# Selective scans on one core: Gelu and Silu on clear steps, A loaded among the scans, seven of 24 products on GpSimd

## The chip, the core and the metric

The kernel runs on one core of a Trainium2 chip. The metric is the device time of one execution in microseconds (us); lower is better. The engines are named as in the profile: PE (TensorE), DVE (VectorE), ACT (ScalarE), POOL (GpSimd) and SP (SyncE, which here only issues transfers).

## The reference

Eight images of 56 x 56 positions with 192 channels go through four layers. Layer 0 splits the channels: one half goes through three convolutions, the other through a layer norm, a projection, a depthwise convolution with Silu and a selective scan in four directions, then a gate and a projection. Layers 1 and 2 are selective scans in four directions with a layer norm. Layer 3 is a shifted-window attention with an MLP (Gelu). What takes the time is the scan, which all of layers 0 to 2 have, for each of 4 directions, 192 channels d and 16 states n:

```
delta = softplus(dts @ dt_proj + bias)                     # per channel and position
h = exp(delta * A) * h + (delta * u) * B                   # A = -exp(A_logs), per (d, n)
y = sum over n of h * C        + D * u
```

## The kernel before

**Units and steps.** A unit is one direction of one layer of one image over a chunk of 784 positions (CK); each image and layer has 4 x 4 of them, 384 in all. Inside a unit, 192 channels x 16 states are cut into 24 steps, each one tile of 128 partitions (32 channels x 4 states) x 784 positions: two halves of the channels (h), four groups of states (sg), three groups of channels (j). So there are 9216 steps, and `s % 24` says where in its unit a step is, `s % 12` where in its half.

**One step.** All engines' work is written out in one loop in `run` (the calls are recorded through wrappers, so nearly all instructions carry line L109). For step t:

- `make`: ACT writes exp(delta * A) into `ps_x`, one of two PSUM tiles, from `dsp` (delta spread over the states); POOL writes `db` = `usp` x `bt`, one of four tiles.
- one iteration later, DVE does the scan along the positions. Its initial value is a column of `state`. In most steps the result goes back into `ps_x`, and DVE multiplies it by `ct` (C) into `hc`. In the other steps, which I call product steps, the scan's result goes straight into `hc`.
- two iterations after `make`, ACT copies the last column of the scan's result into `state`, and in product steps POOL multiplies `hc` by `ct` in place. POOL's product therefore stands in its queue behind the `db` of two steps later, and it overwrites a tile that ACT's copy has to have read.
- after every third step PE sums the three `hc` over the states into `ps_y` (`add_up`). In step 5 of each half ACT copies `ps_y` of the half before into the sum over directions (`merge`, the copy act<-ps_y).

In the kernel before, the product steps are every fourth: t % 4 == 3, six of 24.

**Preparing a half.** `prepare` works out delta for the next half of 12 steps: PE multiplies, ACT applies softplus to two tiles of 392 positions, POOL multiplies delta by u into `du`, SP spreads both over the states into `dsp` and `usp`.

**Tables.** Exp and Ln are in one set of tables on ACT; Softplus, Gelu and Silu are each in another. So each softplus, Gelu or Silu has a table load ahead of it and one behind it (`use_ln_exp`). `table_time` holds these tasks until a step where they may be issued; before, those are the steps with s % 4 in (1, 2).

**Other work.** Everything else (the convolutions, norms, attention and MLP) is written as generators in three queues: `ahead` (`prepare`), `urgent` (norms and projections between layers) and `back` (the front of the next image, the attention of the last). After each step's own instructions the loop takes pieces of `ahead` as far as they go, then of `urgent`, then of `back`, as long as an estimated budget of PE and ACT time per step (SPARE, MOST) isn't used up. When a half or a chunk is needed at once, `need` forces the queues. The order on each engine is the order of these calls; no scheduler changes it.

**Start and end.** `constants` loads the constants before anything else. A of the three layers is loaded there by 48 DMAs on POOL's queue (L264), and ACT (L268) and DVE (L269) turn each into -exp(A_logs). After the last scan the attention of the last image runs alone.

Of the kernel before, what the change touches and what calls it, by code (L numbers as in the profile page):

```python
# [32 lines left out]
AF = mybir.ActivationFunctionType  # L33
# [19 lines left out]
NSG = N // SN  # L53
NG = C // G * NSG
# [84 lines left out]
class Net:  # L139
# [56 lines left out]
    def constants(self, ctx):  # L196
        nc, cp = self.nc, self.cp
        self.vt = self.const("vec", [CH, NV])
        self.ident = cp.tile([128, 128], F32, name="ident")
        make_identity(nc, self.ident)  # L200
        self.ones = cp.tile([CH, CH], F32, name="ones")
        nc.vector.memset(self.ones, 1.0)
        self.eps = cp.tile([128, 1], F32, name="eps")
        nc.vector.memset(self.eps, EPS)
        self.blk = self.const("blk", [CH, CH])
        self.esum = cp.tile([128, G], F32, name="esum")
        nc.vector.reduce_sum(
            self.esum, self.ident.rearrange("p (d n) -> p d n", n=SN), axis=AX.X
        )


        self.wx = []
        for l in range(3):
            R = RANK[l]
            wx = cp.tile([CH, 2, 2, 4 * N + 2 * R], F32, name=f"wx{l}")
            for k in range(K):
                d, at = k // 2, 4 * N + k // 2 * R
                src = self.a[f"wx{l}"][:, :, k, :]
                nc.sync.dma_start(
                    out=wx[:, :, k % 2, 2 * N * d : 2 * N * d + 2 * N], in_=src[:, :, R:]  # L220
                )
                nc.scalar.dma_start(out=wx[:, :, k % 2, at : at + R], in_=src[:, :, :R])
                for c in range(2):
                    at = VAT[f"dtb{l}"] + c * K + k
                    nc.gpsimd.dma_start(
                        out=self.dtw[:1, l, k, CH * c : CH * c + CH],
                        in_=self.a["vec"][:, at : at + 1].rearrange("p o -> o p"),
                    )
            self.wx.append(wx)
            nc.sync.dma_start(out=self.dtw[1 : 1 + R, l], in_=self.a[f"dtw{l}"])  # L230

        with self.tc.tile_pool(name="setup", bufs=1) as sp:

            rstd = sp.tile([CH, 3], F32, name="rstd")
            at = VAT["bn1_v"]
            nc.scalar.activation(rstd, self.vt[:, at : at + 3], AF.Sqrt, bias=self.eps[:CH])
            nc.vector.reciprocal(rstd, rstd)
            self.bns = cp.tile([CH, 3], F32, name="bns")
            self.bnb = cp.tile([CH, 3], F32, name="bnb")
            at = VAT["bn1_g"]  # L240
            nc.vector.tensor_mul(self.bns, self.vt[:, at : at + 3], rstd)
            t = sp.tile([CH, 3], F32, name="bnt")
            at = VAT["bn1_m"]
            nc.vector.tensor_copy(t, self.vt[:, at : at + 3])
            for i in (1, 2):
                nc.vector.tensor_sub(t[:, i : i + 1], t[:, i : i + 1], self.v(f"conv{i}_b"))
            nc.vector.tensor_mul(t, t, self.bns)
            at = VAT["bn1_b"]
            nc.vector.tensor_sub(self.bnb, self.vt[:, at : at + 3], t)


            self.dsum = dsum = cp.tile([CH, 3, 2], F32, name="dsum")
            self.A = []
            for l in range(3):
                at = VAT[f"D{l}"]
                d = self.vt[:, at : at + 2 * K].rearrange("p (c k) -> p c k", k=K)
                nc.vector.reduce_sum(dsum[:, l, :], d, axis=AX.X)
                A = cp.tile([128, K, C // G, NSG], F32, name=f"A{l}")
                src = self.a[f"A{l}"].rearrange(
                    "(d s n) (k j q) -> q s d n k j", s=NSG, n=SN, k=K, q=4  # L260
                )
                for q in range(4):
                    for sg in range(NSG):
                        nc.gpsimd.dma_start(  # L264
                            out=A[32 * q : 32 * q + 32, :, :, sg], in_=src[q, sg]
                        )
                A = A.rearrange("p k j s -> p (k j s)")
                nc.scalar.activation(A, A, AF.Exp)  # L268
                nc.vector.tensor_scalar_mul(A, A, -1.0)  # L269
                self.A.append(A)  # L270


            ls = sp.tile([CH, 2], F32, name="ls")
            at = VAT["ls"]
            nc.vector.tensor_scalar_min(ls, self.vt[:, at : at + 2], math.log(100.0))
            nc.scalar.activation(ls, ls, AF.Exp)
            self.scm = cp.tile([CH, 2, 3], F32, name="scm")
            at = VAT["hm"]
            for c in range(2):
                nc.vector.tensor_scalar_mul(  # L280
                    self.scm[:, c, :], self.vt[:, at : at + 3], ls[:, c : c + 1]
                )
            self.ln1024 = cp.tile([CH, 1], F32, name="ln1024")
            nc.vector.memset(self.ln1024, 10.0 * math.log(2.0))

    def l3_constants(self):

# [105 lines left out]
    def table_time(self):  # L393


        while self.step % 4 not in (1, 2) and not self.forced:
            yield 1

    def other_table(self, func, *tiles):
# [415 lines left out]
    def run(self):  # L815
        nc = self.nc
# [13 lines left out]
        for i in range(NC):  # L830
            self.urgent.append(Task(self.after(-1, i)))
        self.urgent.append(Task(self.columns(0)))
        self.state = self.s1.tile([128, NG], F32, name="state")
        self.B_, self.C_, self.spread = {}, {}, {}

# [2 lines left out]
        ]  # L838
        S = len(steps)
        half = NG // 2  # L840
        self.step = 0
        self.ahead.append(Task(self.prepare(units[0], 0, 0)))
        self.need(("half", 0))
        self.ahead.append(Task(self.prepare(units[0], 1, half)))
        for sg in range(NSG):
            self.load_bc(units[0], sg)
        made, weighed, copies = {}, {}, deque()
        left = dict.fromkeys(self.load, 0.0)
        for s in range(S + 8):
# [5 lines left out]
            t = s + half + 1  # L855
            if t < S and t % half == 0:
                self.ahead.append(Task(self.prepare(*steps[t][:2], t)))
            if s < S and s % half == 0:
                self.need(("half", s))
                U = steps[s][0]  # L860
                if s % (16 * NG) == 0:
                    if U.l == 0:
                        self.begin_image(U.b)
                    self.dd = self.s1.tile([CH, 2, CH], F32, name="dd")
                    for c in range(2):
                        nc.scalar.activation(
                            self.dd[:, c, :], self.ident[:CH, :CH], AF.Copy,
                            scale=self.dsum[:, U.l, c : c + 1],
                        )

            t = s - 2
            if 0 <= t < S and not steps[t][0].last:
                U, h, sg, j = steps[t]
# [5 lines left out]
            t = s - 1  # L879
            if 0 <= t < S:  # L880
                U, h, sg, j = steps[t]
                x, db = made[t]
                pool = t % 4 == 3
                hc = self.s6.tile([128, CK], F32, name="hc")
                hs = hc if pool else x
                sense = slice(None) if U.k < 2 else slice(None, None, -1)
                nc.vector.tensor_tensor_scan(
                    hs[:, sense], x[:, sense], db[:, sense],
                    0.0 if U.first else self.at_state(h, sg, j), ALU.mult, ALU.add,
                )  # L890
                if not pool:
                    nc.vector.tensor_mul(hc, hs, self.C_[U, sg])
                made[t] = hs
                weighed[t] = hc
            t = s - 2
            if 0 <= t < S and t % 4 == 3:
                U, h, sg, j = steps[t]
                nc.gpsimd.tensor_mul(weighed[t], weighed[t], self.C_[U, sg])
            t = s - 4
            if 0 <= t < S and t % 3 == 2:  # L900
                U, h, sg, j = steps[t]
# [6 lines left out]
            while self.piece(self.ahead):  # L908
                pass
            self.spend(left, before)  # L910
            for queue in (self.urgent, self.back):
                while min(left["PE"], left["ACT"]) > 0.0 and self.piece(queue):
                    before = self.spend(left, before)

            t = s - 4
            if 0 <= t < S and t % NG >= half and t % 3 == 2:
                n = t // NG + 1
# [484 lines left out]
MOST = {"PE": 3.4, "ACT": 2.5, "DVE": 1.6, "POOL": 3.0}  # L1402


def view(t, k, c, i, n):

    if k % 2 == 0:
        return t[:, c, i : i + n]
    return t.rearrange("p c (h w) -> p c w h", w=HW)[:, c, i // HW : (i + n) // HW, :]
# [120 lines left out]
```

## Time and profile before

| | |
|---|---|
| median of 3 runs | 27071.03 us (27067.4 to 27074.87) |
| the profiled execution: its own time | 27060.61 us |
| its span (first to last instruction) | 27058.8 us |
| busy share: DVE, POOL, PE, ACT | 89%, 85%, 68%, 64% |
| first scan starts, last scan ends | 181.1 us, 26410.6 us |
| mean granted PE clock | 0.756 |

A group of instructions in the profile reads: line, engine, operation, tiles written <- tiles read, sizes, count | busy us in all, mean ns of one | idle us of the engine just before them, and what ended most of that idle time. A wait reads: waiting engine and tile <- what it waited for: us in total, times, longest us. In the timeline each line has the start, the length, and in brackets the idle time ahead of it.

### The profile page before, as it was taken

The page shows a single profiled execution, that of the slowest core. Times are in us where ns is not written, and L with a number is a line of the kernel's source. Part 1 is how long each engine was busy: PE and PEld are TensorE (multiplying, and loading weights), DVE is VectorE, ACT ScalarE, POOL GpSimd, SP SyncE. Part 2 cuts the span into 40 slices and gives each one's busy share as a digit, 9 for nine tenths or more (in the row PEclk, how much of TensorE's full clock was granted, in tenths as well). Part 3 has the DMA queues.
Part 4 walks back from the last instruction along what each step waited for, and adds up shares of the span by engine and source line. Part 5 has one row for each costly group of instructions (what it writes and reads, how often), then busy time and mean ns, then how long its engine had stood idle before and what let it go on. Part 6 is the DMA issues. An engine that isn't in the chain of part 4 may idle for free. (4 is left out here: it accounts for less than half of the span.)

```text
span 27058.8 us, 260255 instructions
## 1 busy us (share of the span) xinstructions
PE 18495.3 (68%) x76788; PEld 6432.0 (24%) x76788; DVE 24122.4 (89%) x18972; ACT 17211.8 (64%) x30893; POOL 23054.4 (85%) x13199
## 2 busy tenths in 40 slices
PE   6675567676676666766667676677766776676657
PEld 2221122222222222222222222222212222222114
DVE  5999999999999899999999999989999899999991
ACT  4655566665666666666666666666666666666655
POOL 5888988888888888888888888888888888888991
PEclk7776677777777777777777777777777777777777
DMA  4555565556555565555655556555565555555550
GB/s 96 135 138 124 133 136 133 126 127 139 135 132 127 125 144 132 132 126 129 142 131 132 127 131 140 133 129 127 131 140 131 129 128 135 134 129 129 130 132 25
DMA packets 1503447, 3472.21 MB, mean 128 GB/s; under 512 B 310618, under 2 KB 503219, under 8 KB 1502020
## 3 DMA queue, kind: packets, MB, share of 16 engines
q1 hardware_dynamic: 1496452, 3455.15, 56.0%
q8 instruction: 606, 9.93, 0.1%
q0 software_dynamic: 3072, 0.31, 0.1%
q14 instruction: 821, 6.73, 0.1%
q10 hardware_dynamic: 2496, 0.09, 0.0%
HBM read 1457.23 MB, written 147.89 MB: 59 GB/s over the span
## 5 line engine op out<-in xcount | busy, mean ns | idle before, releaser
L109 POOL TENSOR_TENSOR db<-usp,bt 128x784 f32<-128x784 f32 x9216 | 16832.7, 1857 | 161.8 <-DMA usp<-du 129.3
L109 DVE TENSOR_TENSOR_SCAN ps_x<-ps_x,state,db 128x784 f32<-128x784 f32 x5184 | 9569.7, 1846 | 834.0 <-ACT state L109 358.7
L109 ACT ACTIVATE ps_x<-dsp,A 128x784 f32<-128x784 f32 x9216 | 8464.1, 919 | 2496.9 <-DVE hc L109 2190.5
L109 PE MATMUL ps_y<-hc,esum 128*32 128x392 f32 x36864 | 6959.3, 641 | 1147.3 <-POOL hc L109 780.6
L109 DVE TENSOR_TENSOR hc<-ps_x,ct 128x784 f32<-128x784 f32 x6912 | 6739.5, 975 | 651.4 <-DVE ps_x L109 11.0
L109 POOL TENSOR_TENSOR hc<-hc,ct 128x784 f32<-128x784 f32 x2304 | 4254.4, 1847 | 2696.2 <-ACT state L109 2104.5
L109 ACT COPY state<-ps_x 128x1 f32<-128x1 f32 x5184 | 831.4, 160 | 4659.5 <-DVE hc L109 4637.4
L109 DVE TENSOR_TENSOR_SCAN hc<-ps_x,state,db 128x784 f32<-128x784 f32 x1728 | 3181.7, 1841 | 161.6 <-POOL db L109 58.2
L109 DVE TENSOR_TENSOR_SCAN ps_x<-ps_x,db 128x784 f32<-128x784 f32 x1728 | 3085.0, 1785 | 261.1 <-ACT state L109 149.1
L109 PEld LDWEIGHTS ps_y<-hc,esum 128*32 128x32 f32 x36864 | 1630.6, 130 | 6096.7 <-issue 3212.3
L109 PE MATMUL ps_y<-act,ident 96*96 96x392 f32 x2304 | 1612.2, 835 | 1760.4 <-ACT act L109 1746.4
L109 PE MATMUL ps_p<-act,act 13*96 13x392 f32 (+1 forms) x3072 | 1513.0, 605 | 1116.6 <-ACT s L109 210.4
L109 POOL TENSOR_TENSOR du<-delta,act 96x784 f32<-96x784 f32 x768 | 1567.9, 2042 | 201.3 <-ACT delta L109 198.7
L109 PE MATMUL ps_p<-act,wx 96*88 96x392 f32 (+1 forms) x1536 | 985.8, 778 | 686.9 <-ACT delta L109 394.0
L109 ACT ACT_TABLE_LOAD x896 | 1149.6, 1283 | 34.4 <-PE ps_p L109 18.9
L390 ACT ACT_TABLE_LOAD x897 | 1150.9, 1283 | 15.6
L109 PEld LDWEIGHTS ps_y<-act,ident 96*96 96x96 f32 x2304 | 465.0, 223 | 2603.1 <-ACT act L109 2056.6
L109 DVE TENSOR_TENSOR_SCAN hc<-ps_x,db 128x784 f32<-128x784 f32 x576 | 1025.8, 1781 | 58.8 <-ACT state L109 38.0
L109 PEld LDWEIGHTS ps_p<-act,act 13*96 13x96 f32 (+1 forms) x3072 | 465.4, 180 | 2033.6 <-issue 373.5
L109 ACT COPY act<-ps_y 96x784 f32<-96x784 f32 x768 | 928.0, 1208 | 8.5 <-PE ps_y L109 8.5
L109 PE MATMUL ps_p<-xip,diag 96*96 96x448 f32 x2016 | 864.0, 580 | 94.4 <-ACT delta L109 94.3
L109 ACT COPY state<-hc 128x1 f32<-128x1 f32 x1728 | 328.6, 190 | 883.6 <-DVE hc L109 880.4
(212 smaller groups left out, 18126.0 us busy)
## 6 DMA issues: line engine op xcount, KB each, us to landing
dsp<-delta SPq DMA_DIRECT2D x2304, 392.0 KB
usp<-du SPq DMA_DIRECT2D x2304, 392.0 KB
bt<-bcd SPq DMA_DIRECT2D x1536, 392.0 KB
ct<-bcd SPq DMA_DIRECT2D x1536, 392.0 KB
wf<-in_wf SPq DMA_DIRECT2D x128, 288.0 KB
wf<-wf2d SPq DMA_DIRECT2D x128, 288.0 KB
bcd<-bcx SPq DMA_DIRECT2D x256, 134.8 KB
szd<-sz SPq DMA_DIRECT2D x56, 336.0 KB
```

The lines of the kernel that those rows point to most:

```text
L109: return call(out, *args, **k)
L390: self.tc.nc.scalar.preload_act_table_set(LN_EXP)
```

## The change

Three things are changed together.

- **A.** Only layer 0's A is loaded in `constants`, by 16 DMAs on ACT's queue; its exp and sign (`decay`) come just ahead of the first exp of a scan. The loads of the other two, 32 DMAs, are a task in `urgent` (`decays`), four at a time on SP's queue, followed by the same exp and sign.
- **Products.** The product steps are seven of 24: t % 24 in (2, 6, 9, 13, 16, 20, 23).
- **Steps for tables.** A step is clear if neither it nor the one before is a product step and it isn't step 5 of its half. Softplus may be issued on clear steps; Gelu and Silu on clear steps that aren't among the first three of a half. While a softplus waits for its step, no piece of `urgent` and `back` is taken; in the iteration after one in which a Gelu or Silu waited, `back` is taken ahead of `urgent`.

```diff
-                for q in range(4):
-                    for sg in range(NSG):
-                        nc.gpsimd.dma_start(
-                            out=A[32 * q : 32 * q + 32, :, :, sg], in_=src[q, sg]
-                        )
-                A = A.rearrange("p k j s -> p (k j s)")
-                nc.scalar.activation(A, A, AF.Exp)
-                nc.vector.tensor_scalar_mul(A, A, -1.0)
-                self.A.append(A)
+                self.logs.append([
+                    (A[32 * q : 32 * q + 32, :, :, sg], src[q, sg])
+                    for q in range(4) for sg in range(NSG)
+                ])
+            for out, part in self.logs[0]:
+                nc.scalar.dma_start(out=out, in_=part)
...
+    def decay(self, l):
+
+        self.nc.scalar.activation(self.A[l], self.A[l], AF.Exp)
+        self.nc.vector.tensor_scalar_mul(self.A[l], self.A[l], -1.0)
+        self.done.add(("A", l))
+
+    def decays(self, l):
+        for n, (out, part) in enumerate(self.logs[l]):
+            self.nc.sync.dma_start(out=out, in_=part)
+            if n % 4 == 3:
+                yield 1
+        yield 4
+        self.decay(l)
...
-        while self.step % 4 not in (1, 2) and not self.forced:
+
+        ahead = self.rank == 2
+
+        def clear(s):
+            late = s % (NG // 2) == 5 or not ahead and s % (NG // 2) < 3
+            return not (late or products(s) or products(s - 1))
+
+        while not self.forced and not clear(self.step):
+            if ahead:
+                self.quiet = self.step
+            else:
+                self.wanted = self.step
             yield 1
...
+        for l in (1, 2):
+            self.urgent.append(Task(self.decays(l)))
...
         self.need(("half", 0))
+        self.decay(0)
...
+                    self.need(("A", U.l))
...
-                pool = t % 4 == 3
+                pool = products(t)
...
-            if 0 <= t < S and t % 4 == 3:
+            if 0 <= t < S and products(t):
                 U, h, sg, j = steps[t]
                 nc.gpsimd.tensor_mul(weighed[t], weighed[t], self.C_[U, sg])
...
-            for queue in (self.urgent, self.back):
-                while min(left["PE"], left["ACT"]) > 0.0 and self.piece(queue):
+            both = self.urgent, self.back
+            for queue in both[::-1] if self.wanted == s - 1 else both:
+                while min(left["PE"], left["ACT"]) > 0.0 and self.quiet < s and self.piece(queue):
...
+def products(t):
+
+    return t % 24 in (2, 6, 9, 13, 16, 20, 23)
```

More of the change, by code (lines that the diff above doesn't have):

```diff
@@ L252, in constants @@
             self.dsum = dsum = cp.tile([CH, 3, 2], F32, name="dsum")
-            self.A = []
+            self.A, self.logs = [], []
             for l in range(3):
@@ L258, in constants @@
                 A = cp.tile([128, K, C // G, NSG], F32, name=f"A{l}")
+                self.A.append(A.rearrange("p k j s -> p (k j s)"))
                 src = self.a[f"A{l}"].rearrange(
@@ L840, in run @@
         half = NG // 2
-        self.step = 0
+        self.step, self.quiet, self.wanted = 0, -1, -1
         self.ahead.append(Task(self.prepare(units[0], 0, 0)))
         self.need(("half", 0))
+        self.decay(0)
         self.ahead.append(Task(self.prepare(units[0], 1, half)))
```

## The prediction

> **What bounds the kernel now.** I read the busy line of the page first, then busy time by stretch, then the costliest groups, then the timeline of a quiet stretch, and last the waits of VectorE (DVE), GpSimd (POOL) and ScalarE (ACT). The busy line:
>
> ```profile
> PE 18495.3 (68%) x76788; PEld 6432.0 (24%) x76788; DVE 24122.4 (89%) x18972; ACT 17211.8 (64%) x30893; POOL 23054.4 (85%) x13199
> ```
>
> Busy time by stretch (DVE, ACT and POOL are the third to fifth figures after the length); the first scan starts at 181 us, the last ends at 26410.6:
>
> ```profile
> 0.00:182.00 182.00, 65.47 (x132) 24.72 (x132) 9.75 (x57) 53.65 (x105) 65.62 (x89) 0.82 0.35 48
> 500.00:26411.00 25911.00, 17761.60 (x72959) 6064.67 (x72958) 23856.51 (x18598) 16653.52 (x29556) 22764.07 (x12938) 0.76 0.58 132
> 26411.00:27058.00 647.00, 462.49 (x3096) 270.95 (x3096) 76.56 (x168) 357.84 (x967) 53.64 (x65) 0.77 0.10 26
> ```
>
> So there is a head of 181 us, a loop of 26229 us with 9216 steps (2.846 us each), and a tail of 647 us. In the loop DVE is busy 92% and POOL 88%: a change that hands work from one to the other can swap the bound. The groups it moves:
>
> ```profile
> L109 POOL TENSOR_TENSOR db<-usp,bt 128x784 f32<-128x784 f32 x9216 | 16832.7, 1857 | 161.8 <-DMA usp<-du 129.3
> L109 DVE TENSOR_TENSOR hc<-ps_x,ct 128x784 f32<-128x784 f32 x6912 | 6739.5, 975 | 651.4 <-DVE ps_x L109 11.0
> L109 POOL TENSOR_TENSOR hc<-hc,ct 128x784 f32<-128x784 f32 x2304 | 4254.4, 1847 | 2696.2 <-ACT state L109 2104.5
> L109 POOL TENSOR_TENSOR du<-delta,act 96x784 f32<-96x784 f32 x768 | 1567.9, 2042 | 201.3 <-ACT delta L109 198.7
> ```
>
> DVE's timeline in a stretch without a wait (start, length):
>
> ```profile
> 13020.55 1.85 DVE L109 TENSOR_TENSOR_SCAN ps_x<-ps_x,state,db 128x784 f32<-128x784 f32 x1
> 13022.51 0.97 DVE L109 TENSOR_TENSOR hc<-ps_x,ct 128x784 f32<-128x784 f32 x1
> 13023.40 1.85 DVE L109 TENSOR_TENSOR_SCAN ps_x<-ps_x,state,db 128x784 f32<-128x784 f32 x1
> ...
> 13026.24 1.84 DVE L109 TENSOR_TENSOR_SCAN hc<-ps_x,state,db 128x784 f32<-128x784 f32 x1
> 13028.00 1.83 DVE L109 TENSOR_TENSOR_SCAN ps_x<-ps_x,state,db 128x784 f32<-128x784 f32 x1
> ```
>
> A step whose product stays on DVE takes 2.84 us there (13020.55 to 13023.40), one whose product goes to POOL 1.76 us (13026.24 to 13028.00). At that pace the loop would take 6912 x 2.84 + 2304 x 1.76 = 23690 us; 2540 us are lost. Some 440 us of that are DVE's other work, about 1570 us waits (its idle of 2218 us in the loop less 6912 x 0.094 us of turnaround before products), the rest lost overlap around them. DVE's longest waits in the loop, then POOL's:
>
> ```profile
> DVE ps_x L109 <- ACT state L109: 414.5, 295, 5.4
> DVE ps_x L109 <- ACT ps_x L109: 336.8, 240, 5.2
> DVE ps_x L109 <- POOL db L109: 148.8, 65, 14.2
> POOL hc L109 <- ACT state L109: 1981.3, 1105, 6.3
> ```
>
> DVE waits mostly for ACT, which is late with the next exp. POOL waits 1981 us before its products for the copy of a state out of the same tile: there it is ahead and is held to DVE's pace.
>
> What makes ACT late is shown best by a Gelu that falls in the step of a merge copy; ACT, then DVE:
>
> ```profile
> 4853.15 0.81 ACT L109 COPY act<-ps_y 96x784 f32<-96x784 f32 x1
> ...
> 4856.36 2.17 ACT L109 ACTIVATE hid<-hid 128x2352 f32<-128x2352 f32 x1
> 4858.54 1.28 ACT L390 ACT_TABLE_LOAD   x1
> 4859.84 1.76 ACT L109 ACTIVATE ps_x<-dsp,A 128x784 f32<-128x784 f32 x2
> ```
> ```profile
> 4860.86 1.86 DVE L109 TENSOR_TENSOR_SCAN ps_x<-ps_x,state,db 128x784 f32<-128x784 f32 x1 [4.59 <-ACT ps_x L109]
> ```
>
> I sorted the scans' waits for ACT by what ACT had run in the 7 us before: 191 us in 55 waits had a Gelu, 82 us in 49 a Silu, 93 us in 66 a softplus in a merge copy's step, 118 us another softplus, 521 us none of these (about 100 us of it before 430 us).
>
> **Two rules of the Trainium skill.** "ScalarE: Activation LUTs", What ACT_TABLE_LOAD costs: a switch of table is a load of about 1283 ns and a drain of about 1380 ns. The load agrees (1283 ns mean of both table groups), the drain doesn't show: at 4858.54 the load starts as the Gelu ends, and the exp follows its end by 0.02 us. I go by the trace: Gelu 4.76 us with both loads, Silu 4.18, softplus 3.48. "GPSIMD Engine Reference", Specifications: GpSimd shares SBUF interfaces with VectorE, and contends with VectorE instructions that have two SBUF inputs. The scans and products here read one tensor in PSUM and one in SBUF, and the change adds no others; POOL's product ranges only from 1825 to 1985 ns. So I leave all durations as they are.
>
> **The change, part by part.** The sum is made against the profiled execution, 27060.6 us (span 27058.8); the median of the runs is 10 us above it, and I add those at the end.
>
> *A among the scans.* 48 loads of A on POOL's queue (46.7 us at 0.98 each) go; ACT waits for them until 63 us, and its chain to the first scan starts only then. In their place are 16 loads on ACT's queue. The nearest row is ACT's loads of wx, 0.62 us each: 10 us, so ACT is free at about 22 us instead of 63: -40. Bounds: with 2.5 us per load (four times wx's pieces) nothing is gained. The other 32 are issued by SP behind about 100 scans, up to 12 in a row between dsp and usp; SP issues about one DMA a step (10683 in all) at 0.5 to 2 us each, and what is late behind them is the next usp or bt: between 0 and 30 us, +10. The three exps (0.28 us) and products (0.21 us) of A are moved, not added; each stands on ACT four steps or more behind its loads, so the exps queued behind it have nothing to wait for.
>
> *Seven products in 24 steps.* The step pattern becomes 2, 6, 9, 13, 16, 20, 23. DVE: 384 steps go from 2.84 to 1.76 us: -415. (In busy time 384 x 0.975 = 374.)
>
> POOL gets 384 products of 1.80 us from start to start: +691. It had 26229 - 22940 = 3290 us idle in the loop, so most of it fits, but not all. Per 24 steps the clean pace is: DVE 17 x 2.84 + 7 x 1.76 = 60.6; POOL 31 x 1.82 + 2 x 2.2 (du) = 60.8, and its other work 1.5 (DVE's other work 1.1). Today it is 61.7 against 59.0. POOL can't build up a lead: its product of step p stands behind db of p+2 and waits for the scan of p, so it has two dbs in hand there, no more. In a stretch of four steps between products it needs 9.1 us and DVE 10.3; in the new stretches of three 7.3 against 7.4, and with a du 9.5. The built order puts 308 du into the stretch 23-2 and 212 into 13-16 (softplus on steps 1 and 15), 156 behind step 13 and 76 behind 5, in stretches of four. With softplus on step 1, counted from the start of scan 0: the product of 23 ends at 2.1, db 2 at 3.9, du at 6.1, db 3 at 7.9; scan 2 starts at 5.7 and, as its product is POOL's, scan 3 could start at 7.4. Today that scan has 1.05 us in hand in the median (and under 0.12 in 14%), with a step of 2.84 ahead; it loses 1.08. So half of these 520 stretches begin to wait: about 0.3 us on average, 156 us. As much again for POOL's 576 small products (0.64 to 0.97 us) and DMA waits, whose slack goes in the stretches of three: +300 in all. Bounds: 0 (DVE's ACT waits give POOL the time anyway) to +700 (every POOL microsecond shows).
>
> *Gelu and Silu on clear steps.* No product starts there, no merge copy, and softplus's own steps are left out. On a clear step two full steps (5.68 us) pass between the exp ahead of the event and the scan that needs the next exp; less exp, state copy and exp (0.92 + 0.16 + 0.92) that leaves 3.68 us: softplus (3.48) fits, Silu exceeds it by 0.5 and Gelu by 1.1. In the built order the events in a merge copy's step fall from 105 (23 Gelu, 81 softplus) to 1, and those one step behind another from 46 to 14. Gelu: 191 to 56 x 1.1 = 62: -130. Silu: 82 to 37: -45. Softplus off step 5: -80. Together -255; bounds -100 to -330. Back work that is held while a softplus waits comes later in the same 24 steps; eight Gelus lie behind the last scan in both programs, so the tail is not longer. If that cover is gone, PE and ACT get bunched work: up to +100, in the range.
>
> Sum: -40 + 10 - 415 + 300 - 255 = -400: 26660.6, with the 10 us 26670.
>
> **Rivals.** (1) *All of it comes through*: POOL's new work hides wholly, as its 12% idle suggests: 26370. Against it: equal clean paces. (2) *The transfer cancels itself*: the DVE gain of 415 comes back as waits for db (+700): 27070. (3) *POOL becomes the bound and ends slower*. Its place is the product that waits for the state copy: 2000 us of idle that POOL needs to stay behind DVE and ACT. If the idle doesn't shrink, the loop grows by all 691 us, less 40: 27720. The time is 691 - 40 less what the idle shrinks by: my sum needs it to shrink by 1050 (3290 to 2240); under 590 the kernel is slower. For it: seven synchronisations instead of six; against it: six in ten of these waits end with POOL ahead, and a slower POOL simply waits less. (4) *The change doesn't do what it says*: the built order shows the steps as named above, so I give it nothing.
>
> **Numbers.** A measurement of this kernel tells 0.2% (54 us) from no change. My case 0.68, its own range 26400 to 27000; rival 1 0.10; rival 2 0.10; rival 3 0.12. Below 27017: my case and rival 1, with the edge of both: 0.80; within 0.2% 0.08; slower 0.12. The range 26330 to 27070 takes in rival 1 and the near side of rival 2.
>
> **What would show it.** First scan near 141 us. DVE busy near 23750, POOL near 23710. POOL's wait for state copies down from 1981 us to about 1100; DVE's waits for db up from 225 us to about 500; its waits for ACT down by 250, none of 4 us behind a Gelu. I am wrong if DVE waits for db over 900 us, if POOL's idle stays above 2600, or if the first scan doesn't move.

## The result: 1.3% slower, and the profile after

The changed kernel takes 27418.95 us (median of 4 runs, 27409.67 to 27423.9) against 27072.95 for the kernel before: ratio 1.013, 95% interval 1.0113 to 1.0146. The prediction was 26670, and its range ended at 27070. The profiled execution of the changed kernel has a span of 27407.3 us; its first scan starts at 144.0 us and its last ends at 26755.6.

The busy line, and busy time by stretch (head, loop, tail; DVE, ACT and POOL are the third to fifth figures after the length):

```profile
PE 18596.9 (68%) x76788; PEld 6535.9 (24%) x76788; DVE 23809.3 (87%) x18588; ACT 17085.8 (62%) x30893; POOL 23713.7 (87%) x13535
```
```profile
0.00:145.00 145.00, 64.43 (x132) 24.56 (x132) 9.44 (x55) 52.83 (x103) 18.85 (x41) 0.78 0.30 57
500.00:26756.00 26256.00, 17832.38 (x72834) 6159.02 (x72834) 23507.82 (x18193) 16509.28 (x29530) 23427.04 (x13298) 0.74 0.56 130
26756.00:27407.00 651.00, 463.40 (x3096) 271.05 (x3096) 76.71 (x168) 356.81 (x967) 53.62 (x65) 0.77 0.10 26
```

DVE lost 313 us of work and POOL gained 659, about as planned, and both now stand at 87%. The head is 37 us shorter, the tail 4 longer. The loss is in the loop: 26612 us instead of 26229. The groups that were to move kept their durations (975, 1845, 2038 ns); what changed is the idle time ahead of them:

```profile
L109 POOL TENSOR_TENSOR db<-usp,bt 128x784 f32<-128x784 f32 x9216 | 16868.1, 1857 | 351.3 <-DMA usp<-du 296.5
L109 DVE TENSOR_TENSOR hc<-ps_x,ct 128x784 f32<-128x784 f32 x6528 | 6364.9, 975 | 611.8 <-DVE ps_x L109 15.6
L109 POOL TENSOR_TENSOR hc<-hc,ct 128x784 f32<-128x784 f32 x2688 | 4959.7, 1845 | 2164.2 <-ACT state L109 1718.9
L109 POOL TENSOR_TENSOR du<-delta,act 96x784 f32<-96x784 f32 x768 | 1565.4, 2038 | 335.4 <-ACT delta L109 262.1
```

POOL's wait for usp ahead of db rose from 129 to 296 us. In the loop alone DVE's longest waits are these, and ACT's and PE's that matter here:

```profile
DVE ps_x L109 <- POOL db L109: 479.5, 488, 8.4
DVE ps_x L109 <- ACT ps_x L109: 434.8, 225, 10.1
DVE hc L109 <- ACT state L109: 333.5, 253, 7.3
...
DVE hc L109 <- POOL db L109: 70.4, 50, 7.2
```
```profile
ACT bcx L109 <- PE ps_p L109: 613.8, 169, 12.6
ACT ps_x L109 <- DMA dsp<-delta: 341.4, 221, 6.9
```
```profile
PE ps_p L109 <- DMA act<-u0d: 489.9, 28, 19.6
```

DVE waits 550 us for db instead of 225. The lines of ACT and PE were 152, 102 and 190 us in the kernel before: late loads, and a copy of ACT's (`bcx`) behind one of them. The loop can be split as in the prediction. From scan to scan a step still takes 2.84 us in the median with its product on DVE and about 1.76 without (1.757 before, 1.765 now); at that pace the loop would take 23270 us, 415 less than before, and what is lost beyond that rose from about 2540 to 3340.

**Where the stall behind u0 comes from.** In the loop u0, the input of the next image, is loaded 28 times. In the kernel before, every one of these loads was followed by two or three steps with a softplus in them, and only then by the projection that reads it; in the changed kernel none is. Kernel before, timeline (SPq is SP's queue), then the changed kernel:

```profile
9963.60 0.57 SPq L713 DMA_DIRECT2D act<-u0d  x1
...
9966.88 0.88 ACT L109 ACTIVATE delta<-ps_p 96x392 f32<-96x392 f32 x2
...
9969.68 2.86 PE L109 MATMUL ps_p<-act,wx 96*76 96x392 f32 x4 [8.88 <-DMA act<-u0d]
...
9972.58 0.48 ACT L109 COPY bcx<-ps_p 76x392 f32<-76x392 f32 x1 [1.24 <-PE ps_p L109]
```
```profile
10049.28 0.58 SPq L736 DMA_DIRECT2D act<-u0d  x1
10055.08 2.87 PE L109 MATMUL ps_p<-act,wx 96*76 96x392 f32 x4 [18.07 <-DMA act<-u0d]
...
10057.99 0.48 ACT L109 COPY bcx<-ps_p 76x392 f32<-76x392 f32 x1 [11.97 <-PE ps_p L109]
...
10059.48 1.86 DVE L109 TENSOR_TENSOR_SCAN ps_x<-ps_x,state,db 128x784 f32<-128x784 f32 x1 [9.77 <-ACT state L109]
```

The load takes 5.8 us from issue to the first matmul in the second case. What differs is what ACT has queued: before, three exps and a softplus; after, the copy `bcx` stands next in the queue, and the state copy and exp that the scan needs stand behind it. DVE stood idle for over 8 us ahead of a scan 10 times before and 33 times after. In 28 of the 33 the cause is such a load, at the end of layer 2, where the next image's input comes in. Together these 28 stalls last 270 us.

### The profile page after: what moved, and what is told of

Its sections match the earlier page's. It is cut to its first block, busy times and chain, and to the rows that moved or that the text cites. A ratio compares the mean times of both kernels' runs of the same rounds, so it can differ in the third digit from the quotient of the medians.

```text
span 27407.3 us, 260324 instructions
## 1 busy us (share of the span) xinstructions
PE 18596.9 (68%) x76788; PEld 6535.9 (24%) x76788; DVE 23809.3 (87%) x18588; ACT 17085.8 (62%) x30893; POOL 23713.7 (87%) x13535
## 5 line engine op out<-in xcount | busy, mean ns | idle before, releaser
L109 POOL TENSOR_TENSOR db<-usp,bt 128x784 f32<-128x784 f32 x9216 | 16868.1, 1857 | 351.3 <-DMA usp<-du 296.5
L109 DVE TENSOR_TENSOR_SCAN ps_x<-ps_x,state,db 128x784 f32<-128x784 f32 x4896 | 9038.8, 1846 | 1005.5 <-POOL db L109 376.6
L109 PE MATMUL ps_y<-hc,esum 128*32 128x392 f32 x36864 | 6837.1, 634 | 1097.7 <-POOL hc L109 666.5
L109 DVE TENSOR_TENSOR hc<-ps_x,ct 128x784 f32<-128x784 f32 x6528 | 6364.9, 975 | 611.8 <-DVE ps_x L109 15.6
L109 POOL TENSOR_TENSOR hc<-hc,ct 128x784 f32<-128x784 f32 x2688 | 4959.7, 1845 | 2164.2 <-ACT state L109 1718.9
L109 DVE TENSOR_TENSOR_SCAN hc<-ps_x,state,db 128x784 f32<-128x784 f32 x2016 | 3714.9, 1843 | 368.2 <-ACT state L109 202.6
L109 DVE TENSOR_TENSOR_SCAN ps_x<-ps_x,db 128x784 f32<-128x784 f32 x1632 | 2914.8, 1786 | 328.1 <-ACT ps_x L109 163.9
L109 POOL TENSOR_TENSOR du<-delta,act 96x784 f32<-96x784 f32 x768 | 1565.4, 2038 | 335.4 <-ACT delta L109 262.1
L109 DVE TENSOR_TENSOR_SCAN hc<-ps_x,db 128x784 f32<-128x784 f32 x672 | 1197.7, 1782 | 151.7 <-ACT state L109 138.4
L109 ACT COPY state<-hc 128x1 f32<-128x1 f32 x2016 | 384.0, 190 | 785.0 <-DVE hc L109 779.3
```

The costliest lines, as they stand in the source:

```text
L109: return call(out, *args, **k)
```

## The experiments

All ratios are against the kernel before, measured alongside (27055 to 27073 us).

**A alone (e4).** The kernel before with the part on A and nothing else.

> The kernel before with the first part of the change alone (A loaded on ACT's queue and among the scans). Both theories: first scan at 144 us instead of 181, the loop as before: 27036 us. If the 32 loads on SP's queue delay dsp and usp, up to 30 us of that is lost: 27066.

Measured: 27049.62 us, ratio 0.9996 (0.9987 to 1.0005). The first scan starts at 142.5 us, but the loop is 20 us longer, so some 10 of the 38 us reach the end, less than a measurement tells.

**The hold and the load of u0 (e1, e3).** I call it the hold that other work is kept back while a softplus waits. e1 takes the hold away; e3 keeps it and puts three iterations between the load of u0 and its reader.

```diff
# e1
-                while min(left["PE"], left["ACT"]) > 0.0 and self.quiet < s and self.piece(queue):
+                while min(left["PE"], left["ACT"]) > 0.0 and self.piece(queue):
# e3, in after(), behind the DMA out of u0
+                if g >= 0:
+                    yield 3
```

> The changed kernel, but other work is no longer held while a softplus waits for its step. Theory S (the hold moved the u0 loads behind the softplus, so ACT's copy of the projection stands right behind a load that has not landed; 26 stalls of about 9.8 us = 255 us): in the built order 12 of 28 copies again have a softplus ahead of them, so about 12 x 9 = 110 us come back: 27310 us, and about 14 stalls over 8 us instead of 29. Rival P (seven products make POOL the bound): no change, 27420. Rival H (the hold protects the softplus from work ahead of it on ACT): slower, 27500 or more.

> The changed kernel with three iterations between the issue of a u0 load and the projection that reads it. Theory S: the 10 us stalls behind the 28 loads go, -230 us: 27190 us; ACT's wait of bcx for PE falls from 670 us to about 220. Rival P: nothing changes, 27420 us, since DVE's waits for db stay at 568 us.

Measured: e1 27266.05 us, 1.0076 (1.0061 to 1.0091); e3 27250.37 us, 1.0069 (1.0054 to 1.0084). Against the changed kernel e1 gains 153 us and e3 169. In e3 the gaps over 8 us fall from 33 to 5; of the 270 us of stalls, 100 come back as other waits or lost overlap. In e1 12 of the 28 loads have a softplus behind them again, as foreseen, but 16 stall as before, and 26 gaps over 8 us are left, not about 14: some 120 us of its gain are the 12 stalls, the rest has no account. So the hold isn't alone in taking the cover away. The new steps for softplus do it too: in e5 below, which has no hold, 22 of the 28 loads stall.

**Six against seven products (e2, e6, e5).** e2 is the changed kernel with `t % 4 == 3`, e6 is e2 with e3's three steps, e5 is the kernel before with seven products and a table rule to fit, without hold and without the part on A. The rule for tables looks at the product steps, so e2 and e6 also move softplus, Gelu and Silu to other steps.

```diff
# e2, e6
-    return t % 24 in (2, 6, 9, 13, 16, 20, 23)
+    return t % 4 == 3
```

> The changed kernel with the six product steps of before (every fourth). Theory S: the stalls behind the u0 loads stay (the copy follows the load with no softplus between), DVE has 384 more steps of 2.84 instead of 1.76 us (+415), its waits for db fall from 568 us to about 250: 27420 + 415 - 320 = 27510 us. Rival P: the seventh product is what costs; six bring the time to that of before less the earlier start, 27040 us or less.

> The changed kernel with six product steps and three iterations between a u0 load and its projection: both suspected losses are undone, the earlier start and the steps for Gelu and Silu stay. Theory M with S: 27198 less 20 to 28 stalls of 9 us = 26980 us, faster than the kernel before by 0.3%. Rival R (the hold itself costs): 27060 or more.

> The kernel before with the seven product steps alone; tables on any step that neither is nor follows a product step (the rule of before, carried over to the new pattern), no hold, A as before. Theory M (the seventh product costs more than it saves: DVE saves 415 us of steps, but waits for db and for late dsp grow by more): 27060 + 210 = 27270 us, DVE's waits for db over 480 us, ACT's waits for dsp over 300. Rival Q (the product move gains and the rules for the tables lose): 26800 us or less.

Measured: e2 27198.28 us, 1.005 (1.0033 to 1.0067); e6 27035.29, 0.9989 (0.9982 to 0.9995); e5 27336.72, 1.01 (1.0085 to 1.0115). With u0's stall and without it, the kernel with seven products takes 215 to 221 us more than the one with six. In e2 DVE's scans wait 170 us for db instead of 568 (whole execution), POOL for usp 125 instead of 296, ACT for dsp 120 instead of 358. But the scans' waits with a Gelu ahead fall as well, from 191 to 94 us, because the table rule gives Gelu other steps: the 220 us are not the seventh product's alone. e2 lies between its two forecasts, e6 55 us above its own and e5 67 above its nearer one.

In e6 the scans' waits with a Gelu ahead are 95 us instead of the 191 of the kernel before and those with a Silu 19 instead of 82, yet with A the whole gains only 27 us: the waits without a table event at the steps around a merge copy rose from about 45 to 130.

**POOL later, or loads earlier (e7, e9, e10, e16).** A ring is the set of tiles that a name uses in turn. e7 issues POOL's product one iteration later. e9 (on e3) and e10 (on e6) give usp and dsp rings of five tiles, and let the loads for j = 1 and 2 be issued a step earlier; e16 is e10 with the hc ring back at eight.

```diff
# e7
-            t = s - 2
+            t = s - 3
             if 0 <= t < S and products(t):
# e9, e10 (e16: HCS = 8 and bcx from s1)
-        delta = self.s2.tile([CH, CK], F32, name="delta")
+        delta = self.s1.tile([CH, CK], F32, name="delta")
...
-            while j and self.step < start - 4 + j:
+            while j and self.step < start - 5 + j:
...
-                s = self.s4.tile([128, CK], F32, name=name)
+                s = self.spreads[name].tile([128, CK], F32, name=name)
...
-HCS = 8
+HCS = 7
```

> The changed kernel with POOL's product issued one iteration later, behind db of three steps ahead instead of two. Theory L (POOL is held to DVE with two dbs in hand at every product, and is late after each): one more db in hand, DVE's waits for db fall from 568 to about 250 us and ACT's for dsp from 358 to about 150: 27170 us. Rival W (POOL has too much work whatever its order, and PE now waits longer for hc): DVE's waits for db stay over 450, PE's waits for hc rise above 667 us, the time is 27420 or more.

Measured: 27641.22 us, 1.0209 (1.0193 to 1.0224). The signs of rival W came (DVE's scans wait 818 us for db, PE 1527 for POOL's hc). But what POOL lacks first isn't time: now with three dbs in hand, it gets to a db sooner and finds its usp not there. These waits are from the whole execution of e7:

```profile
POOL db L109 <- DMA usp<-du: 1127.6, 386, 9.4
```

The theory that POOL needs a longer lead fell. What counts is when these loads are issued. With rings of four, the loads for j = 1 and 2 of the next half take tiles that the current half frees in its steps 9 and 10, four steps ahead of their use. The changed kernel's timeline shows such loads; the first line is POOL's db of steps 21 and 22, and the usp at 14803.10 is that for j = 2:

```profile
14794.12 3.66 POOL L109 TENSOR_TENSOR db<-usp,bt 128x784 f32<-128x784 f32 x2
...
14797.22 1.43 SPq L1049 DMA_DIRECT2D dsp<-delta  x1
...
14798.70 1.09 SPq L807 DMA_DIRECT2D bcd<-bcx  x1
...
14799.84 2.51 SPq L1001 DMA_DIRECT2D bt<-bcd  x1
14802.45 0.55 SPq L1001 DMA_DIRECT2D ct<-bcd  x1
14803.10 0.55 SPq L1049 DMA_DIRECT2D usp<-du  x1
...
14803.74 0.56 SPq L1049 DMA_DIRECT2D dsp<-delta  x1
...
14810.27 5.55 POOL L109 TENSOR_TENSOR db<-usp,bt 128x784 f32<-128x784 f32 x3 [2.34 <-DMA usp<-du]
...
14811.26 1.75 ACT L109 ACTIVATE ps_x<-dsp,A 128x784 f32<-128x784 f32 x2 [2.70 <-DMA dsp<-delta]
```

From issue to use it is 7.2 us, and both POOL and ACT stand idle for it: 209 of the 384 units have such a wait of POOL at step 2, 79 before. The tile itself was free at 14797.78, when POOL had ended the db of step 22. SP, which issues in the order of the program, came to the load 5.3 us later: ahead stood the dsp for j = 1, a store of `bcx`, and `bt` and `ct` (B and C for the next unit). I compared, for each of the 240 late loads of usp for j = 2, its issue with the end of the db that frees its tile: the issue comes 4.2 us later in the median, and `bt` and `ct` take 3.1 us of that on average. The loads for j = 1 do go out as soon as their tile is free (0.03 us), and only 10 of them are late. So what makes a load late is mostly its place in SP's queue, not the ring.

> Base: e3 (seven products, projection three steps after its load of u0; 27250, +188 over before). Here usp and dsp have rings of five tiles instead of four (delta one instead of two, hc seven instead of eight, to make room), and a spread load j may be issued a step earlier. Theory L2 (the seventh product costs time because the loads of usp and dsp for j = 2 come late: their slot is freed by the db and exp of the half before, only two or three steps ahead): POOL's waits for usp fall from about 300 us to under 120, ACT's for dsp from about 360 to under 120, and the time falls by 120 us or more, to 27130 or below. Theory B (POOL's stretch of three steps with du is too short for its work, whoever frees a tile): usp and dsp waits fall, but DVE's waits for db stay above 450 us and the time stays within 60 us of 27250.

> Base: e6 (six products, projection three steps after u0; 27035, -27 against before). The same larger rings. Theory L2: with six products these waits are small (about 125 us each), so at most 60 us are gained: 26975 to 27035. Theory B: within 30 us of 27035. If the smaller hc ring costs anything, it shows here as more than 27065.

Measured: e9 27053.99 us, 0.9997 (0.9989 to 1.0006), 196 less than e3. e10 27058.43, 1.0 (0.9991 to 1.0008), no gain against e6 (23 us more). The db group of e3, then of e9:

```profile
L109 POOL TENSOR_TENSOR db<-usp,bt 128x784 f32<-128x784 f32 x9216 | 16863.4, 1856 | 344.3 <-DMA usp<-du 273.4
```
```profile
L109 POOL TENSOR_TENSOR db<-usp,bt 128x784 f32<-128x784 f32 x9216 | 16867.6, 1857 | 77.3 <-DVE ps_x L109 43.5
```

The waits for usp are gone, and ACT's for dsp (354 us) with them. So late loads are what cost these 196 us, and theory L2 held for seven products in that; its reason, the tile freed too late, holds for few of them. In e9 the load for j = 2 goes out in the median 11.6 us ahead of its use instead of 7.2. Ring and place in the queue were changed together; a run with rings of four and the loads moved ahead of `bt` and `ct` wasn't made. DVE's scans still wait 416 us for db in e9 (536 in e3), under B's 450. With six products the smaller hc ring seems to have cost what the loads brought (e10, waits of DVE), and e16 shows what stood in its place (waits of ACT):

```profile
DVE hc L109 <- PE ps_y L109: 291.0, 115, 6.6
```
```profile
ACT bcx L109 <- DMA bcd<-bcx: 278.6, 75, 9.8
```

> As e10 (six products, larger rings; 27058) with the hc ring back at eight (bcx one tile instead of two to make room). DVE's wait for PE's ps_y (291 us in e10, about 2 in e6) goes: 26900 to 27000 if nothing else takes its place, within 30 us of 27058 if DVE then waits for ACT instead. Set beside e13 it tells whether seven products are worth more than six once loads, u0 and events are seen to: theory B (POOL short of time) says six stay even or ahead, the clean count of DVE says seven by 100 or more.

Measured: 27146.01 us, 1.0036 (1.0023 to 1.0049), a miss: the wait for ps_y went (2 us), but with one tile `bcx` waits for the store of the one before. So what larger rings alone are worth to six products stays open.

**POOL's time (e11, e12).** The same pair, seven on e3 and six on e6, with the du product left out and usp loaded from delta.

```diff
...
-                    nc.gpsimd.tensor_mul(
-                        like(du, k), like(delta, k), view(self.bufs[U.g % 2], k, h, i * CK, CK)
-                    )
...
```

> Base: e3 with seven products. The du product (768 of 2.04 us on POOL) is left out: usp is loaded from delta. Its purpose is the difference to the next run. Theory B (POOL lacks time: 31 db or C products of 1.82 and two du in 60.6 us): without du POOL needs 56.4 us per 24 steps against DVE's 60.6, so seven products are faster than six by 200 us or more (of the clean 415), where with du they are slower by 215; db waits under 200 us. Theory M (a product on POOL hands over at a price, whatever time POOL has: the scan after it follows 1.76 us behind, ACT and PE have to keep up): seven stay slower than six by over 50 us.

> Base: e6 with six products, du left out in the same way. POOL had time to spare with six, so little is gained: theory B says 26950 to 27035 and seven products below it by 200 us or more; theory M says that this run stays the faster of the two by over 50 us.

Measured: e11 26795.14 us, 0.99 (0.9886 to 0.9915); e12 26889.53, 0.9936 (0.992 to 0.9953). Without du seven are 94 us faster than six, with it 215 slower: du's 1565 us on POOL turn the sign. Theory M fell. B's size (200 or more) wasn't reached, and e12 came out 60 us below its forecast; e11 kept late loads (POOL waits 324 us for usp) and dear Gelus (214 us of waits, 97 in e12).

**Where the table events stand (e8, e13, e14, e15).** e8 is the changed kernel with Gelu and Silu also kept off steps 4 and 22; e13 is e9 with 4, 11 and 22; e14 also keeps softplus off 12; e15 is e13 without the hold. The comments in the edit are mine.

```diff
# e13, in clear()
             late = s % (NG // 2) == 5 or not ahead and s % (NG // 2) < 3
+            late |= not ahead and s % NG in (4, 11, 22)      # e8: (4, 22)
# e14:       late |= s % NG in ((12,) if ahead else (4, 11, 22))
```

> The changed kernel, Gelu and Silu also kept off steps 4 and 22 of a unit. Theory G (a Gelu on step 4 has a merge copy in the next step, on 22 a product step next, and loses 5 us there, 1.5 on other clear steps): Gelu's waits fall from 191 to about 100 us; 12 of the 28 u0 loads get two steps by this order, -100 us: 27220 us. Rival (Gelu's cost doesn't depend on the step): Gelu's waits stay at 190, 27320 us from the u0 loads alone.

Measured: 27285.66 us, 1.0083 (1.0066 to 1.0099): 133 less than the changed kernel, between the two forecasts. Gelu's waits fell from 191 to 131 us, and the gaps over 8 us from 33 to 22, so part of the gain is u0's.

The changed kernel with a Gelu on step 4 (ACT, then DVE), and e13 with one on step 18:

```profile
4875.82 0.92 ACT L109 ACTIVATE ps_x<-dsp,A 128x784 f32<-128x784 f32 x1
...
4878.54 0.59 ACT L109 ACTIVATE hid<-ps_p,f1b 128x392 f32<-128x392 f32 x1 [1.80 <-PE ps_p L109]
4879.85 0.59 ACT L109 ACTIVATE hid<-ps_p,f1b 128x392 f32<-128x392 f32 x1 [0.73 <-PE ps_p L109]
4880.46 1.28 ACT L109 ACT_TABLE_LOAD   x1
4881.75 2.16 ACT L109 ACTIVATE hid<-hid 128x2352 f32<-128x2352 f32 x1
...
4885.42 0.92 ACT L109 ACTIVATE ps_x<-dsp,A 128x784 f32<-128x784 f32 x1
...
4886.44 1.80 DVE L109 TENSOR_TENSOR_SCAN ps_x<-ps_x,db 128x784 f32<-128x784 f32 x1 [5.11 <-ACT ps_x L109]
```
```profile
5340.65 0.93 ACT L109 ACTIVATE ps_x<-dsp,A 128x784 f32<-128x784 f32 x1
...
5341.60 1.28 ACT L109 ACT_TABLE_LOAD   x1
5342.90 2.17 ACT L109 ACTIVATE hid<-hid 128x2352 f32<-128x2352 f32 x1
...
5347.40 1.86 DVE L109 TENSOR_TENSOR_SCAN ps_x<-ps_x,state,db 128x784 f32<-128x784 f32 x1 [2.77 <-ACT ps_x L109]
```

In the first, the exp of the step ends at 4876.74, but ACT then stands twice for PE's last products of `hid` (1.80 and 0.73 us) and comes to the Gelu's table load only at 4880.46: the scan needs an exp that follows the Gelu, and waits 5.11 us. Of the lead of two full steps on which the prediction counted, 3.7 us are gone before the event starts. In the second, the exp stands between the last `hid` and the Gelu, and the wait is 2.77.

> Base: e9 (seven products, larger rings, projection three steps after u0; 27054). Here Gelu and Silu also keep off steps 4, 11 and 22 of the 24. Theory G (where a table event stands decides its price in the seven-product pattern): in e9 Gelu costs 6.2 us x 14 on step 4, 4.6 x 12 on 22, 4.2 x 7 on 11, Silu 9.7 x 16 on 11, in all about 325 us; on 8 and 18 they cost 1.5 to 3.2 us each, about 105. Up to 220 are gained, half of that if part of the price was backlog of their steps: 26835 to 26945. Theory N (with a seventh product the slack is gone everywhere, so an event costs the same wherever it stands): within 60 us of 27054.

> As e13, and softplus keeps off step 12 (it goes to 15). In e9 a softplus on 12 cost 1.4 us, one on 15 0.8: theory G says 189 of them gain about 110 us over e13. Theory L (the loads of dsp and usp behind the softplus come later and are what counts): POOL's and ACT's waits for usp and dsp come back and it is slower than e13 by over 50 us.

> As e13, without the hold of the other work while a softplus waits for its step. With u0's loads already three steps ahead: if the hold cost nothing besides the u0 stalls (as e1's and e3's equal times suggest), within 40 us of e13; if bunched work behind the hold costs too, faster by over 60 us; if the hold keeps softplus off a busy ACT, slower.

Measured: e13 26948.98 us, 0.9958 (0.9943 to 0.9973), 105 less than e9, 4 us outside theory G's range and well outside theory N's; Gelu's waits fell from 189 to 111 us. e15 26954.55, 0.9961 (0.9946 to 0.9975), the same: where u0's load has its time, the hold costs nothing. e14 27306.87, 1.009 (1.0075 to 1.0105), a miss by both theories. Its layer periods (384 steps each) add up to 15065 us over the second to fifteenth of the 24 scan layers, against 15179 in e13, and to 9124 against 8767 over the next eight; usp and dsp are not late there. What shows in those eight layers is DVE waiting 185 us for PE ahead of the convolutions' tile `xl`, against 21 in all of e13. Why the convolutions come to stand there wasn't found.

**Which seven steps (e17, e18).** e17 is e13, e18 the changed kernel, each with only this edit:

```diff
-    return t % 24 in (2, 6, 9, 13, 16, 20, 23)
+    return t % 24 in (3, 6, 9, 13, 17, 20, 23)
```

In the changed kernel 215 us of the scans' 568 us of waits for db stand at step 3, 84 at 14 and 74 at 17. One of them (DVE's scans and POOL):

```profile
8000.31 1.84 POOL L109 TENSOR_TENSOR db<-usp,bt 128x784 f32<-128x784 f32 x1
8002.12 1.83 POOL L109 TENSOR_TENSOR du<-delta,act 96x784 f32<-96x784 f32 x1
...
8003.92 1.97 POOL L109 TENSOR_TENSOR act<-act,aux 96x392 f32<-96x392 f32 x2
...
8005.85 3.72 POOL L109 TENSOR_TENSOR db<-usp,bt 128x784 f32<-128x784 f32 x2
8007.76 1.86 DVE L109 TENSOR_TENSOR_SCAN ps_x<-ps_x,state,db 128x784 f32<-128x784 f32 x1 [3.45 <-POOL db L109]
```

Between two products POOL has du and two small products of a gate besides its dbs; the scan behind the product step 2 waits 3.45 us. The table rule follows the pattern here too, so the events move with it.

> As e13 with the seven products on steps 3, 6, 9, 13, 17, 20, 23 instead of 2, 6, 9, 13, 16, 20, 23: the stretches in which du of a softplus on step 1, 12 or 15 falls are now four steps long (23 to 3 and 13 to 17). POOL's and DVE's work is the same in number. Theory B1 (the short stretches with du make POOL late): DVE's waits for db fall from about 400 us to under 200 and the time by 100 to 200 us, to 26750 to 26850. Theory B2 (POOL's total is the limit: 60.8 us against 60.6 of DVE per 24 steps): the waits move to other steps, their sum stays above 350 us, the time within 60 us of 26949. The table rule follows the pattern, so softplus, Gelu and Silu move too (Gelu to 8, 15, 16 and 19): a slower run with more waits for ACT would be theirs.

> The changed kernel (27419) with the seven products on steps 3, 6, 9, 13, 17, 20, 23. If the short stretches with du cost by themselves what e17 against e13 showed (128 us), 27250 to 27330. If the late loads of usp and dsp (196 us by e9) hit in the old pattern only because POOL and ACT had to hurry at step 2, they go as well: 27050 to 27150, with waits for usp and dsp under half of 296 and 358 us. If they stay first in line whatever the pattern, DVE gains nothing: within 60 us of 27419.

Measured: e17 26821.35 us, 0.9916 (0.9899 to 0.9932), 128 less than e13: the waits at step 3 fall from 117 to 6 us, those for db in all from 396 to 286, not to under 200, since some come back at steps 10 and 13 to 18. The gain is net of what the moved events and loads cost: the scans' waits for ACT rise from 791 to 984 us, ACT's for dsp from 7 to 189. In DVE's list of waits (whole execution) ACT stands first again:

```profile
DVE ps_x L109 <- ACT ps_x L109: 317.0, 228, 34.7
DVE ps_x L109 <- ACT state L109: 233.9, 158, 41.6
DVE ps_x L109 <- POOL db L109: 219.8, 194, 14.0
```

e18 27348.16, 1.0108 (1.0092 to 1.0125): 71 less than the changed kernel, just short of the first expectation. The waits at step 3 go there as well (215 to 21), but those for usp and dsp rise to 398 and 547 us: with the loads late, part of what the pattern gives is taken by them.

e17 is the fastest of all: the three parts of the change, with u0's projection three steps behind its load, rings of five, table events off three steps, and products two of which stand one step later. The steps to it, each on the last: 27419, e3 27250, e9 27054, e13 26949, e17 26821. What a step gains depends on what was mended before it: the same new pattern gave 71 us in e18 and 128 in e17.

## Why the prediction was wrong, step by step

- **DVE, -415: right.** The lengths of a clean step stayed, and 384 of them became 1.08 us shorter: the loop at the clean pace fell from 23685 to 23270 us.
- **Waits for db, +300: right in size.** 225 to 550 us in the loop. The place was right too (half of it at steps 3 and 17), and the waits at step 3, which go in e17 and e18, show the short stretches with du as a cause; with du left out (e11) they come to 156 us in all.
- **A, -40 + 10: right at the first scan (-37), too much in the whole.** e4 gained 10 us, by an interval that includes no gain. The products of A counted as "moved, not added" didn't keep their time: two of the three took 2.52 and 2.98 us on DVE instead of 0.21. At 5 us in all this decides nothing here.
- **"Back work that is held while a softplus waits comes later in the same 24 steps": the step that failed.** The sum put moving softplus and holding other work at nothing, because work was only deferred, with up to 100 us in the range for bunched work. The order counted: the softplus that lay between the load of u0 and its reader as cover came ahead of both. With the hold all 28 loads stall, without it 16 (e1). Giving the reader its time back brings 169 us (e3). The prediction asked what was hidden behind the held work, not what the held work had been hidden behind.
- **Late loads of usp and dsp: missing from the sum, and as dear.** "As much again for POOL's 576 small products and DMA waits" spoke of them as slack in POOL alone, within the 300. They rose by 167 us on POOL and stopped ACT for 341 us instead of 102, and larger rings with an earlier issue gave 196 us back (e9). POOL and DVE, now at nearly equal paces, come to a spread tile when it is just landing, and its load stands in SP's queue behind those of B and C.
- **Gelu, -130: nothing came.** The waits with a Gelu ahead were 191 us before and after. 34 of its 47 waits stand behind steps 4, 11 and 22, which the rule calls clear, and there it cost 4 to 6 us and not 1.1: the rule sees neither PE's `hid` nor how far ahead ACT is. With six products, where the rule gives it steps 6 and 18, they did fall, to 95 (e6).
- **Silu, -45, softplus off step 5, -80: right by themselves** (82 to 18 and 93 to 10), but the scans' waits behind a softplus in other steps rose from 118 to 193, and those for ACT with no table event ahead from 521 to 796. The 270 us of u0's stalls are about all of that last rise.
- **The test of rival 3.** POOL's idle had to shrink by 1050 us and slower began at 590; in the loop it shrank by 323 (3289 to 2966, over the 2600 that the prediction gave as a sign of being wrong). By that rival's count the change is +328; it was +346. This count is nearly an identity (the loop is POOL's busy and idle time), so it says how much, not why: that it comes out is no proof of rival 3. POOL as such wasn't the bound: e17 carries the same POOL work in 600 us less. But that POOL's work matters, e11 and e12 show.

Against -400 in the forecast stand +346, 746 us apart. Undone one after the other: u0 169, loads 196, events 105, together 470. The pattern's 128 don't count toward the gap, since the forecast had put 300 us on waits for db and these came. With some 20 us of A, about 250 us stay without an account, and more if one takes into account that e9 also removes waits for usp and dsp that stood before. The place to look is ACT: in e3 the scans wait 1076 us for it, before it was 1004, and the forecast had it 255 lower.

## What to carry to other kernels

Work that is moved may be the cover of something else: before deferring a piece, list the loads issued ahead of it and what will then stand next to their reader in an in-order queue. When two engines are brought to the same pace, check the loads that feed them first: from the release of a tile to its use there must be time for the load and for what stands ahead of it in the queue that issues it. An even spread of a product over the steps is not an even spread of an engine's work: put the longer stretches where its other instructions fall.

## What the runs showed of the hardware

Loads that spread 32 rows over 128 partitions (392 KB), where an engine waited for them in the changed kernel, took 6.1 us (usp) and 7.0 us (dsp) from issue to use in the median for j = 2, the load of u0 (588 KB) 5.8 us. SP's instruction for usp takes 0.55 us in the median, for `ct` 1.97; an instruction that has to wait for its tile shows the wait as its own length (the dsp at 14797.22 takes 1.43 us and ends 0.07 us behind the exp of step 21, which frees its tile), and how much of the 1.97 is such a wait the profile doesn't tell. The 16 loads of A on ACT's queue took 0.71 to 1.44 us each (median 0.78), 14.7 in all, and the 32 on SP's 0.72 to 2.65 (median 0.80), where the prediction had 0.62. POOL's 128x784 products kept means of 1844 to 1857 ns in the kernel before, the changed one, e3, e9 and e17, at six and at seven of them in 24 steps. DVE's sign change of A (128x96, in place in SBUF) took 0.21 us ahead of the scans and 2.52 and 2.98 us among them, while POOL was at db and du; in the kernel with A alone (e4) it was 0.96 and 3.27.
